# The last two groups of a layer-1 feed-forward issued side by side, the second with its own tiles and PSUM tag

## The chip, the cores and the metric

The kernel runs on one core of one Trainium2 chip. Its engines are TensorE (PE), VectorE (DVE), ScalarE (ACT), GpSimd (POOL) and SyncE (SP)[...]. The metric is the device time of one execution in microseconds, as the median of the runs shown.

## The reference

Two layers, each a graph step and a feed-forward step with a residual, over 32 batches of 512 nodes with 256 features, in float32. The change lies in layer 1's feed-forward and in how it shares time with layer 1's attention. Cut to what matters:

```python
x = x + L0_gnn(layernorm(x), adj)
x = x + L0_ffn(layernorm(x))
x = x + L1_gnn(layernorm(x), adj)      # masked attention, 4 heads of 64, norm per head
x = x + L1_ffn(layernorm(x))

def L1_ffn(x):                          # 8 heads of 64, 64 slices per head
    fx = heads(x @ W_fx.T + b_fx)
    xm = heads(x @ W_x.T + b_x)
    sw = softmax((xm @ W_slice.T + b_slice) / temp)          # nodes x slices
    st = einsum(fx, sw) / (sw.sum(nodes) + 1e-5)             # 64 tokens of 512
    ot = hydra(st)                      # in-projection, convolution, two-way scan,
                                        # gate, RMS norm, out-projection
    out = einsum(ot, sw)                # back to the nodes
    return out @ out_w.T + out_b
```

Every batch is independent of the others; a feed-forward needs the finished attention of its own batch.

## The kernel before

Layer 0 (up to about 2572 us) is untouched. Layer 1 is `layer1_plain`. It has two streams of work, both Python generators whose `yield`s are the points at which the other stream may issue.

**Attention** (`attentions`, L1280): for batch b, `attention(b)` (L1189) is woven with `prepare(b + 1)` (L1121). `prepare` gathers the batch's rows with four indirect DMAs on POOL's queue (L1127), loads and turns the adjacency into a mask (`masks`, L1046), normalizes, transposes (`x3T`), computes the heads (`hp`), adds a bias on POOL (`hv`, L1162) and sends a small row out and back as a broadcast (`own`, L1170 to L1173, SP's queue). `attention` has eight turns; each weighs two heads on DVE (`att`, L1186) and multiplies on PE (`avp`, L1219; `adp`, L1226). Three steps of `norm(b)` (L1254) follow, spread over the next batch's turns; they are DVE work with a power on POOL (L1272).

**Feed-forward** (`mixer(g)`, L1545): a group is two batches, so there are 16 groups, 0 to 15; group 14 is batches 28 and 29, group 15 is batches 30 and 31. For each batch `slices` (L1290) normalizes (`normed`, L1094), transposes (`x4T`), computes logits (`lgp`, L1307), their softmax on ACT and DVE (`sw`, L1308 to L1314), the slice sums (`yTp`, L1319) and the transposed weights (`swp`). Then, for the group, `tokens` (L1330: `uTp`, `rnp`, `uT`) and `scan` (L1355) with its chain `xp`, `bcp`, `dtp`, `zp`, the convolutions and gates, `gp`, `segp`, `mix`, `yp`, `qp`, `y`, `yTp`, `oTp`, `vp`, and for each batch `unslice` (L1534: `outp`, the residual add and the store).

The driver (L1561 to L1569) walks the groups. Each `yield` of a mixer names how many shares of attention work it wants; the shares times `PACE` (1.04 x 2 x 29 / 68 = 0.887) are credited, and for every whole credit one step of attention is issued. The wants of one mixer add up to 68. When attention must wait for a free `x` tile, the credit is cleared. `slices` forces attention on until its own batch is attended. Attention thus runs one or two batches ahead; it ends in group 14, and group 15 has nothing issued beside it.

The order so given is a priority: an instruction whose inputs and tiles are free can be placed in front of one that stands earlier in the program.

All of this uses one SBUF pool, `s1`. Of a mixer's tiles `xn`, `x4T`, `sw`, `uT`, `yT`, `xpad` and `z` have one buffer, `swT` has two, `inner` seven. `v` of a group (L1522) lies in the tag `sw`. In PSUM, pool `p1` has four banks of tag `any`, used by mixers and by `prepare`, and four of tag `pv`, used by `attention`.

Of the kernel before, what the change touches and what calls it, by code (L numbers as in the profile page):

```python
# [8 lines left out]
F32 = mybir.dt.float32  # L9
# [3 lines left out]
AF = mybir.ActivationFunctionType  # L13
# [824 lines left out]
def layer1_plain(tc, ident, eps, x2s, ranks, adj, w, out, over, ps):  # L838
# [35 lines left out]
    with ExitStack() as ctx:  # L874
# [168 lines left out]
        se = ctx.enter_context(tc.tile_pool(name="e1", bufs=2, side="right", reuse_waits="tile"))  # L1043
# [40 lines left out]
        sb = ctx.enter_context(tc.tile_pool(name="s1", bufs=2, reuse_waits="tile"))  # L1084
# [4 lines left out]
        def inner(name):  # L1089
            return sb.tile([P, DI], F32, tag="inner", name=name, bufs=7)  # L1090

        xs, ready, attended, stored = {}, {}, set(), set()

        def normed(xt, xn, name):  # L1094
# [14 lines left out]
        def turned(xn, tag, name, want=None):  # L1109

            xnT = sb.tile([P, DC, N], F32, tag=tag, name=name, bufs=1)
            for c in range(DC):
                pt = psum("any", f"{name}p{c}")
                for t in range(NT):
                    nc.tensor.transpose(pt[:, t * P : (t + 1) * P], xn[:, t, c * P : (c + 1) * P], ident)
                nc.scalar.copy(xnT[:, c, :], pt)
                if c + 1 < DC:
                    yield want
            return xnT

        def prepare(b):  # L1121
# [3 lines left out]
            xt = xs[b] = sb.tile([P, NT, D], F32, tag="x", name=f"x{b}", bufs=AHEAD_X)  # L1125
# [9 lines left out]
            for i, _ in enumerate(edged):  # L1135
                if i < 3 or b not in masked:
                    yield
                if i == 2:
                    normed(xt, xn, f"c{b}")
                    nc.gpsimd.tensor_add(xt, xt, beta.unsqueeze(1).to_broadcast([P, NT, D]))  # L1140
                    yield
            mask = masked.pop(b)
            xnT = yield from turned(xn, "x3T", f"x3T{b}")
# [146 lines left out]
        def slices(b, j, yT, rn):  # L1290


            while b not in attended:
                next(ahead)
            xt = xs[b]
            xn = sb.tile([P, NT, D], F32, tag="xn", name=f"x4{b}", bufs=1)
            normed(xt, xn, f"d{b}")
            yield 5
            xnT = yield from turned(xn, "x4T", f"x4T{b}", 1)
            nc.gpsimd.tensor_add(xt, xt, outb.unsqueeze(1).to_broadcast([P, NT, D]))  # L1300
            sw = sb.tile([P, NT, DI], F32, tag="sw", name=f"sw{b}", bufs=1)
            swT = sb.tile([P, KC, N], F32, tag="swT", name=f"swT{b}")
            yield 2
            for t in range(NT):
                pf = psum("any", f"lgp{b}_{t}")
                for c in range(DC):
                    nc.tensor.matmul(pf, xnT[:, c, t * P : (t + 1) * P], wsl[:, c, :], start=c == 0, stop=c == DC - 1)  # L1307
                nc.scalar.activation(sw[:, t, :], pf, AF.Exp)  # L1308
                nc.vector.tensor_mul(sw[:, t, :], sw[:, t, :], ebsl)  # L1309
                s = sw[:, t, :].rearrange("p (h g) -> p h g", h=H)  # L1310
                st = sb.tile([P, H], F32, tag="sst", name=f"sst{b}_{t}")
                nc.vector.tensor_reduce(st, s, AX.X, ALU.add)  # L1312
                nc.vector.reciprocal(st, st)
                nc.vector.tensor_mul(s, s, st.unsqueeze(2).to_broadcast([P, H, G]))  # L1314
                yield 5 if t + 1 == NT else 1
            for c in range(DC):
                py = psum("any", f"yTp{b}_{c}")
                for t in range(NT):
                    nc.tensor.matmul(py, xn[:, t, c * P : (c + 1) * P], sw[:, t, :], start=t == 0, stop=t == NT - 1)  # L1319
                nc.scalar.copy(yT[:, c, :, j, :], py.rearrange("p (h g) -> p h g", h=H))  # L1320
            for k in range(KC):
                pt = psum("any", f"swp{b}_{k}")
                for t in range(NT):
                    nc.tensor.transpose(pt[:, t * P : (t + 1) * P], sw[:, t, k * P : (k + 1) * P], ident)
                nc.scalar.activation(swT[:, k, :], pt, AF.Identity, accum_out=rn[:, j, k : k + 1])
            nc.vector.tensor_scalar_add(rn[:, j, :], rn[:, j, :], 1e-5)
            nc.vector.reciprocal(rn[:, j, :], rn[:, j, :])
            return swT

        def tokens(g, yT, rn, uT):  # L1330

            pu, pn = psum("any", f"uTp{g}"), psum("any", f"rnp{g}")
            uv, nv = (p.rearrange("p (k j g) -> p k j g", k=KC, j=GB) for p in (pu, pn))
            for k in range(KC):
                for i in range(P // C):
                    half, h = slice(i * C, (i + 1) * C), k * (P // C) + i
                    for c in range(DC):
                        nc.tensor.matmul(uv[half, k], wfxT[:, c, h * C : (h + 1) * C], yT[:, c, h],
                                         start=c == 0, stop=c == DC - 1)
            for k in range(KC):  # L1340
                for i in range(P // C):
                    half = slice(i * C, (i + 1) * C)
                    for j in range(GB):
                        nc.tensor.matmul(nv[half, k, j, :], rn[:, j, k : k + 1].to_broadcast([P, C]), ident[:, half],
                                         start=True, stop=True)
            scale = inner(f"scale{g}")
            nc.scalar.copy(scale, pn)

            for k in range(KC):
                cols = slice(k * GB * G, (k + 1) * GB * G)  # L1350
                nc.vector.scalar_tensor_tensor(uT[:, k, :], pu[:, cols], bfx_eps[:, k : k + 1], scale[:, cols],
                                               ALU.add, ALU.mult)
            nc.vector.tensor_add(uT, uT, bfx.to_broadcast([P, KC, GB * G]))

        def scan(g, uT):  # L1355


            T = GB * G

            def chunks(t):  # L1360
                return t.rearrange("p (k n) -> p k n", k=KC)

            def tok_matmul(p, c0, n):
                for c in range(KC):
                    nc.tensor.matmul(p, uT[:, c, :], inT[:, c, c0 : c0 + n], start=c == 0, stop=c == KC - 1)

            yield 4

            px = psum("any", f"xp{g}")
            for k in range(KC):  # L1370
                for c in range(KC):
                    nc.tensor.matmul(px[:, k * T : (k + 1) * T], inT[:, c, DI + k * P : DI + (k + 1) * P],  # L1372
                                     uT[:, c, :], start=c == 0, stop=c == KC - 1)
            xpad = sb.tile([P, KC, GB, LP], F32, tag="xpad", name=f"xpad{g}", bufs=1)
            nc.gpsimd.memset(xpad[:, :, :, : KW - 1], 0.0)
            nc.scalar.copy(xpad[:, :, :, KW - 1 :], px.rearrange("p (k j l) -> p k j l", k=KC, j=GB))
            pb = psum("any", f"bcp{g}")
            for i in range(2):
                c0 = 2 * DI + i * S
                for c in range(KC):  # L1380
                    nc.tensor.matmul(pb[:S, i * T : (i + 1) * T], inT[:, c, c0 : c0 + S], uT[:, c, :],
                                     start=c == 0, stop=c == KC - 1)
            bpad = sb.tile([S, 2, GB, LP], F32, tag="bpad", name=f"bpad{g}", bufs=1)
            nc.gpsimd.memset(bpad[:, :, :, : KW - 1], 0.0)
            nc.scalar.copy(bpad[:, :, :, KW - 1 :],
                           pb[:S, : 2 * T].rearrange("p (k j l) -> p k j l", k=2, j=GB))

            def conv(src, wts, dst):
                nc.vector.tensor_scalar_mul(dst, src[:, :, 0:G], wts[:, 0:1])
                for q in range(1, KW):  # L1390
                    nc.vector.scalar_tensor_tensor(dst, src[:, :, q : q + G], wts[:, q : q + 1], dst,
                                                   ALU.mult, ALU.add)
# [3 lines left out]
            pd = psum("any", f"dtp{g}")  # L1396
            for j in range(GB):
                for i in range(2):
                    for c in range(KC):
                        nc.tensor.matmul(pd[i * G : (i + 1) * G, j * H : (j + 1) * H],  # L1400
                                         uT[:, c, j * G : (j + 1) * G],
                                         inT[:, c, DT0 + i * H : DT0 + (i + 1) * H],
                                         start=c == 0, stop=c == KC - 1)
# [808 lines left out]
```

## Time and profile before

| | us |
|---|---|
| runs | 4689.87, 4715.24, 4680.16 |
| median | 4689.87 |
| profiled execution | 4695.45 |
| its span, first to last instruction | 4693.7 |
| PE busy in the span | 4097.9 (87%) |
| DVE busy | 3410.9 (73%) |
| ACT busy | 2310.3 (49%) |
| POOL busy | 1747.3 (37%) |

PE is the matmul row; its weight loads are a row of their own and overlap it. A matmul's end is modelled, so a busy PE is not PE at its peak. The granted clock is PE's. "Idle before" in the timeline is the time for which an engine had nothing running ahead of an instruction, with what released it. Three stretches of layer 1's steady part, each about as long as one group takes, look alike:

```profile
4302.00:4435.00 133.00, 123.61 (x729) 73.18 (x728) 94.73 (x200) 63.42 (x162) 38.19 (x28) 0.99 0.18 52
4169.00:4302.00 133.00, 125.69 (x754) 72.90 (x754) 93.49 (x199) 65.78 (x168) 37.66 (x29) 0.99 0.16 50
4036.00:4169.00 133.00, 124.16 (x735) 72.98 (x734) 96.50 (x204) 64.47 (x171) 40.43 (x29) 0.97 0.17 50
```

The columns are the window, its length, the busy time with the number of instructions of PE, weight loads, DVE, ACT and POOL, the granted clock, the DMA engines' mean share and GB/s.

### The profile page before, as it was taken

The numbers are of one execution on the slowest core, as the hardware profiler recorded it, in microseconds if no ns is written. First come the engines' busy times: TensorE is split into PE (matmuls) and PEld (weight loads), VectorE is DVE, ScalarE is ACT, GpSimd is POOL, SyncE is SP. The second block draws the span as 40 slices with busy tenths as digits, with TensorE's granted clock in tenths as the row PEclk, the third lists the DMA queues.
The fourth block names the chain that finished last, engine by engine and source line by source line (L and its number), as shares of the span: only waits on it lengthen the run. The fifth ranks groups of instructions, "written<-read, shape, count | busy, mean of one in ns | idle before, by whom it ended". The sixth has DMA issues, their size and how long they took to land. (4 is left out here: it accounts for less than half of the span.)

```text
span 4693.7 us, 56440 instructions
## 1 busy us (share of the span) xinstructions
PE 4097.9 (87%) x19287; PEld 2514.5 (54%) x19287; DVE 3410.9 (73%) x7232; ACT 2310.3 (49%) x4820; POOL 1747.3 (37%) x2027
## 2 busy tenths in 40 slices
PE   5769887889888899879988899999999999999987
PEld 4545554555555565545554355555555555555555
DVE  6667778777787777867777667777777777777773
ACT  2345555455554555546554444544454554444432
POOL 2363445535456444443443322233333233322220
PEclk8889999999999999989999899999999999999998
DMA  4453445535355343554443211111111111111100
GB/s 123 160 173 104 154 133 165 176 105 163 123 162 173 121 142 107 165 186 143 145 159 113 64 46 45 48 46 52 52 53 55 53 55 55 46 55 55 39 14 15
DMA packets 235101, 474.10 MB, mean 101 GB/s; under 512 B 38299, under 2 KB 114075, under 8 KB 234804
## 3 DMA queue, kind: packets, MB, share of 16 engines
q0 software_dynamic: 80256, 282.38, 19.0%
q1 hardware_dynamic: 154548, 188.02, 12.9%
q8 instruction: 154, 2.52, 0.2%
q14 instruction: 143, 1.17, 0.1%
HBM read 413.16 MB, written 57.16 MB: 100 GB/s over the span
## 5 line engine op out<-in xcount | busy, mean ns | idle before, releaser
L601 PE MATMUL clsp<-xnT,wc 128*128 128x512 f32 x1024 | 530.9, 639 | 92.7 <-ACT cls L603 48.5
L601 PE MATMUL gatep<-xnT,wg 128*128 128x512 f32 x1024 | 505.2, 615 | 32.9 <-ACT gate L603 23.4
L628 PE MATMUL po<-wd,acc 128*128 128x256 f32 x2048 | 456.2, 381 | 20.4 <-DVE xs L630 19.9
L628 PEld LDWEIGHTS po<-wd,acc 128*128 128x128 f32 x2048 | 385.9, 190 | 96.3 <-DVE xs L630 31.8
L1186 DVE SCALAR_TENSOR_TENSOR att<-own,other,mask 128x512 f32<-128x512 f32 x512 | 376.3, 757 | 17.9 <-DMA own<-ownd 16.9
L615 DVE SCALAR_TENSOR_TENSOR acc<-past,fld,acc 128x512 f32<-128x512 f32 x448 | 349.5, 784 | 51.7 <-ACT past L614 38.0
L581 DVE SCALAR_TENSOR_TENSOR best<-rows,xs,best 128x1024 f32<-128x1024 f32 x212 | 276.0, 1304 | 124.5 <-ACT best L575 62.5
L601 PEld LDWEIGHTS gatep<-xnT,wg 128*128 128x128 f32 x1024 | 200.3, 199 | 289.5 <-issue 210.6
L614 ACT ACTIVATE past<-tz,fld 128x512 f32<-128x512 f32 x448 | 293.6, 693 | 97.5 <-DVE acc L615 97.1
L601 PEld LDWEIGHTS clsp<-xnT,wc 128*128 128x128 f32 x1024 | 189.8, 202 | 246.6 <-issue 126.4
L1219 PE MATMUL avp<-att,hv 128*64 128x512 f32 x1024 | 309.8, 628 | 3.3 <-DVE att L1186 3.3
L578 POOL DMA_INDIRECT rows<-table,xs x212 | 253.8, 1197 | 109.4 <-DVE best L581 49.5
L414 PE MATMUL pm<-h,adj 128*128 128x257 f32 x1024 | 268.1, 403 | 28.3 <-DVE u L411 18.5
L1307 PE MATMUL lgp<-wsl,x4T 128*128 128x512 f32 x512 | 253.1, 630 | 33.6 <-DVE mask L1058 26.2
L603 ACT ACTIVATE cls<-clsp,fld 128x512 f32<-128x512 f32 x256 | 176.1, 688 | 215.3 <-PE clsp L601 111.0
L1319 PE MATMUL yTp<-sw,x 128*128 128x512 f32 x512 | 244.1, 617 | 36.8 <-DVE sw L1314 29.6
L1127 POOL DMA_INDIRECT x<-x2s,ranks x128 | 141.3, 1104 | 346.9 <-DVE att L1186 128.5
L617 DVE TENSOR_TENSOR acc<-acc,cls 128x512 f32<-128x512 f32 x256 | 180.6, 707 | 94.3 <-ACT acc L610 88.6
L603 ACT ACTIVATE gate<-gatep,fld 128x512 f32<-128x512 f32 x256 | 175.2, 684 | 149.7 <-PE gatep L601 118.2
L610 ACT ACTIVATE acc<-tz,fld 128x512 f32<-128x512 f32 x256 | 199.0, 779 | 96.4 <-PE tz L608 90.8
L533 POOL DMA_INDIRECT xs<-rows_of,order x128 | 146.5, 1144 | 264.6 <-DVE acc L615 118.3
L414 PEld LDWEIGHTS pm<-h,adj 128*128 128x128 f32 x1024 | 201.1, 202 | 77.8 <-DVE u L411 25.6
(597 smaller groups left out, 8999.1 us busy)
## 6 DMA issues: line engine op xcount, KB each, us to landing
adji<-in_adj SPq DMA_DIRECT2D x128, 256.0 KB, 4.5
ai<-in_adj SPq DMA_DIRECT2D x128, 256.0 KB, 2.7
own<-ownd SPq DMA_DIRECT2D x128, 256.0 KB, 3.7
rows_of<-keep SPq DMA_DIRECT2D x32, 550.0 KB, 6.7
x<-in_x SPq DMA_DIRECT2D x32, 512.0 KB, 7.6
x2s<-xs SPq DMA_DIRECT2D x32, 512.0 KB, 2.9
out<-x SPq DMA_DIRECT2D x32, 512.0 KB, 3.2
rows<-table,xs POOLq DMA_INDIRECT x212, 5.4
```

The costliest lines, as they stand in the source:

```text
L414: nc.tensor.matmul(pm[:, : D + 1], a[:, i, t * P : (t + 1) * P], h[:, i, :], start=i == 0, stop=i == NT - 1)
L578: nc.gpsimd.indirect_dma_start(out=row, out_offset=None, in_=table, in_offset=bass.IndirectOffsetOnAxis(ap=idxs[:, k : k + 1].bitcast(U32) ...
L581: nc.vector.scalar_tensor_tensor(m, row, vals[:, k : k + 1], m, ALU.add, ALU.max)
L601: nc.tensor.matmul(pf, wf[:, c, f * P : (f + 1) * P], xnT[:, c, :], start=c == 0, stop=c == DC - 1)
L603: nc.scalar.activation(o, pf, fn, bias=fld[:, f, bf : bf + 1], scale=1.0 if fn == AF.Gelu else 0.5)
L614: nc.scalar.activation(r, z, AF.Relu, bias=fld[:, f, AT + b : AT + b + 1])
L615: nc.vector.scalar_tensor_tensor(y, r, fld[:, f, CH + b : CH + b + 1], y, ALU.mult, ALU.add)
L628: nc.tensor.matmul(po[:, :D], acc[f][:, t * P : (t + 1) * P], wd[:, f, :], start=f == 0, stop=f == FC - 1)
L1186: nc.vector.scalar_tensor_tensor(e, own[h], other[:, j, h : h + 1], mask[:, j, :], ALU.max, ALU.mult)
L1219: nc.tensor.matmul(pv[q][k * HO : (k + 1) * HO, :], hv[:, j, h, :HO], weighed[b, h, j], start=j == 0, stop=j == NT - 1)
L1307: nc.tensor.matmul(pf, xnT[:, c, t * P : (t + 1) * P], wsl[:, c, :], start=c == 0, stop=c == DC - 1)
L1319: nc.tensor.matmul(py, xn[:, t, c * P : (c + 1) * P], sw[:, t, :], start=t == 0, stop=t == NT - 1)
```

## The change

Four things, all in `layer1_plain`:

1. The pool is split. `s1` (now `sm`) keeps `x` and the mixers' tiles; a new pool `a1` (`sb`) takes attention's. `a1` and the mask pool `e1` are entered on a stack of their own, `early`, which is closed when attention has ended.
2. `slices`, `tokens`, `scan`, `unslice` and `mixer` move into a function `mixers(sb, bank)`, which takes the pool and the PSUM tag; their bodies are the same, with `psum(bank, ...)` for `psum("any", ...)`. `normed` and `turned` get the pool (and the tag) as arguments.
3. In group 14 attention is credited at twice `PACE`. When attention is exhausted, the loop over group 14's steps is left where it stands.
4. Attention's pool is closed, a pool `s2` is opened in its place, and the rest of group 14 is issued step by step in turn with group 15 (`braid`, L90), which uses `s2` and the tag `pv`.

```diff
-        se = ctx.enter_context(tc.tile_pool(name="e1", bufs=2, side="right", reuse_waits="tile"))
+        early = ctx.enter_context(ExitStack())
+        se = early.enter_context(tc.tile_pool(name="e1", bufs=2, side="right", reuse_waits="tile"))
...
-        sb = ctx.enter_context(tc.tile_pool(name="s1", bufs=2, reuse_waits="tile"))
+        sm = ctx.enter_context(tc.tile_pool(name="s1", bufs=2, reuse_waits="tile"))
+        sb = early.enter_context(tc.tile_pool(name="a1", bufs=2, reuse_waits="tile"))
...
-        def slices(b, j, yT, rn):
+        def mixers(sb, bank):
+            def inner(name):
+                return sb.tile([P, DI], F32, tag="inner", name=name, bufs=7)
+            def slices(b, j, yT, rn):
...
-                pf = psum("any", f"lgp{b}_{t}")
+                    pf = psum(bank, f"lgp{b}_{t}")
...
+            return mixer
...
         ahead = attentions()
-        credit = 0.0
-        for g in range(B // GB):
-            for want in mixer(g):
-                credit += want * PACE
-                while credit >= 1.0:
+        credit, over_with = 0.0, object()
+        mixer = mixers(sm, "any")
+        last = B // GB - 1
+        for g in range(last):
+            steps_ = mixer(g)
+            for want in steps_:
+                credit += want * (PACE if g + 1 < last else 2.0 * PACE)
+                state = None
+                while credit >= 1.0 and state is not over_with:
                     credit -= 1.0
-                    if next(ahead, True):
+                    state = next(ahead, over_with)
+                    if state:
                         credit = 0.0
+                if state is over_with:
+                    break
+        for _ in ahead:
+            pass
+        early.close()
+        sm2 = ctx.enter_context(tc.tile_pool(name="s2", bufs=2, reuse_waits="tile"))
+        braid(steps_, mixers(sm2, "pv")(last))
```

`braid` takes one step of each live stream in turn:

```python
def braid(*streams):

    live = [iter(s) for s in streams]
    while live:
        live = [s for s in live if next(s, live) is not live]
```

## The prediction

> **What bounds the kernel now.** I read the windows view first, cut where the trace changes character: start of group 14, last attention transposes, start of group 15's matmuls, its token step, its last matmul. Columns: window, us, then busy us (instructions) of PE, weight loads, DVE, ACT, POOL, then granted clock, DMA share, GB/s.
>
> ```profile
> 4443.00:4536.50 93.50, 87.47 (x491) 43.18 (x489) 73.19 (x163) 39.84 (x91) 23.24 (x18) 1.00 0.07 23
> 4536.50:4580.00 43.50, 31.02 (x185) 27.11 (x186) 21.32 (x37) 8.84 (x19) 8.61 (x5) 0.76 0.04 13
> 4580.00:4616.50 36.50, 33.81 (x95) 15.57 (x94) 17.00 (x35) 12.96 (x27) 2.35 (x1) 0.95 0.04 15
> 4616.50:4679.20 62.70, 50.86 (x373) 42.42 (x371) 17.91 (x54) 21.68 (x41) 0.71 (x1) 0.84 0.03 9
> 4443.00:4679.20 236.20, 203.16 (x1139) 128.28 (x1137) 129.42 (x287) 83.32 (x176) 34.91 (x25) 0.91 0.05 16
> ```
>
> PE is the bound as long as attention runs (87.5 of 93.5 us); after it PE idles 12.5, 2.7 and 11.8 us in the three windows and the clock drops. The timeline of PE shows where:
>
> ```profile
> 4535.26 1.04 PE L1205 MATMUL bp<-ident,avT 128*128 128x128 f32 x8
> 4543.15 3.28 PE L1484 MATMUL yp<-xk,mix 64*64 64x64 f32 x32 [6.85 <-DVE mix L1477]
> ...
> 4553.04 1.08 PE L1499 MATMUL yTp<-ident,y 128*128 128x128 f32 x4 [4.81 <-DVE y L1494]
> 4554.80 6.47 PE L1507 MATMUL oTp<-yT,hoT 128*128 128x128 f32 x32 [0.68 <-ACT yT L1501]
> ...
> 4565.55 14.08 PE L1539 MATMUL outp<-v,swT 128*128 128x256 f32 x64
> ...
> 4580.74 7.13 PE L1307 MATMUL lgp<-wsl,x4T 128*128 128x512 f32 x16 [0.24 <-ACT x4T L1116]
> ...
> 4600.84 8.83 PE L1307 MATMUL lgp<-wsl,x4T 128*128 128x512 f32 x16 [0.57 <-ACT x4T L1116]
> ...
> 4623.82 5.44 PE L1372 MATMUL xp<-uT,inT 128*128 128x128 f32 x32 [2.65 <-DVE uT L1353]
> ```
>
> Two stalls of group 14 (6.85, 4.81) stand bare although group 15's slices were ready: batch 30's statistics ran at 4527. Its logits start only after the last outp: `sw` has one buffer, and `v` of group 14 sits in it until outp has read it. Slow matmuls follow each stall: oTp 6.47 against 3.84 in group 13, xp 5.44 against 3.84 in group 14, the second lgp 8.83 against 7.13. The timeline of DVE shows the other half:
>
> ```profile
> 4477.85 0.26 DVE L1573 TENSOR_TENSOR over<-edges 128x128 f32<-128x128 f32 x1
> ...
> 4538.44 0.68 DVE L1476 TENSOR_TENSOR mix<-mix,back 128x512 f32<-128x512 f32 x1
> 4539.04 1.22 DVE L1262 SCALAR_TENSOR_TENSOR av<-av,ht 128x1024 f32<-128x1024 f32 x1
> 4540.17 2.83 DVE L1477 TENSOR_TENSOR mix<-mix,decay 128x512 f32<-128x512 f32 x1
> ```
>
> L1573 stands last in the program, yet runs at 4478: ready work is pulled into gaps unless tiles hold it back. L1477 takes 2.83 where group 15's takes 0.69; a POOL add (L1300) runs from 4539.03 for 3.42.
>
> **What the Trainium skill says.** "TensorE: Matmul & The Clock Gate", Part 1: an idle window of about 3.4 us halves PE's clock. Agrees: 0.76 in the window with the 6.85 gap. "Perfetto Trace Analysis", Identifying Performance Opportunities: bubbles can mean that the next tile has no buffer. Agrees: `sw`/`v`. The same page, Optimizing Scalar/DVE Operations: GpSimd and DVE share an SBUF read port. Agrees: 2.83 against 0.69. "ScalarE: Activation LUTs", What ACT_TABLE_LOAD costs: 1283 ns plus a drain of about 1380. The trace has 1.28 a load; the next ACTIVATE follows at once, so I price a switch at 1.28.
>
> **The change, part by part.** Loss against warm, gapless PE from 4443 to 4679.2: idle 33.0 (236.2 - 203.2) plus cold excess: oTp 2.6, x4T31 0.9, lgp 1.7, xp 1.6, oTp 2.3, segp and xtp 0.5 = 9.6. So warm PE work is 193.6 and loss 42.6: front 6.0; group 14's tail 12.5 + 2.6 = 15.1; slices 30/31 2.7 + 2.6 = 5.3; group 15's tail 11.8 + 4.4 = 16.2.
>
> *Moved: attention to double pace.* Counting yields, 49 attention steps remain at the start of group 14 in either version. Before, they are spent at `yp y` of group 14; now at its 14th yield, after batch 29's last logits: both slices carry all attention. Rows, 4441 to 4557: att 19.9, av 4.0, three norms 26.5, masks 2.7, statistics 2.4, hv 1.5, small 1.0 = 58.0 DVE; two slices 17.7 + 2.8 = 20.5; batch 27's last adds 1.6, flags 1.4. DVE sum 81.5. PE: avp 18.8, adp 8.5, hp 4.4, transposes 7.0, slices without batch 29's yTp and swp 28: 67; behind the last norm those 9.4 and tokens 3.4 can still go: 80. So **DVE becomes the bound of the front half**. It idled 20.3 of 93.5 before, on batch 31's gather (3.7), the POOL add into `hv` (8.2), POOL powers (4.9), dp (1.8). With more ready work I halve that: 81.5 + 10 = 92, attention over near 4535, front PE idle 12. Ends: 4 (as dense as 4462 to 4478, without a DVE gap) and 22 (all gaps kept, 101.8 - 80). POOL's share (four gathers, two adds of 2.4 to 3.4, pows of 3.3 to 4.4), the mask loads and the `own` write and reads on SP's queue (3.4 + 4.5) crowd into the same stretch: inside those ends.
>
> *Added: second set, `pv` banks, braid.* No instruction is added on PE, DVE or POOL. Group 14's tokens to outp alternate with batch 30's slices and the start of batch 31's. Its 15.1 and the slices' 5.3 should be filled: each gap below 7 us meets a 7 us lgp or yTp of the other stream. I keep 4 (the slices still wait once for their normed x, and norm 31 ends there); ends 1 and 9. ACT switches tables more: up to 8 loads, 10 us, but ACT is busy 9 of 43 us there: nothing on PE; bare, 2.6 us in the 4. The new tiles lie where attention's were and wait for its last readers: norm 31, in front of them in DVE's queue anyway; zero, at most its 2.4 (L1275, L1276). Two out stores of 3.2 us move between the slices on SP; nobody waits for them since no gather is left.
>
> *Kept:* group 15's tail, 16.2; nothing is left to run beside it.
>
> *Elsewhere:* up to group 13 the order is the same by count. The split of one pool in two puts attention's tiles on other addresses, so other tiles of layer 0 hold them back at the border (PE idles 18 us of 2550 to 2600): zero, 5 either way.
>
> Sum: loss after 12 + 4 + 16.2 = 32.2, against 42.6: **10 us less**. The profiled execution was 4695.45 (span 4693.7 and 1.75 around it), 5.6 above the median 4689.87: 4685 there, 4680 as a median.
>
> **Rivals.**
> *Front pays it all*: idle there 18 to 22; gain 0 ± 4: 4690. For: DVE at 81.5 of 92. Against: pulled work as at L1573.
> *Front filled*: idle near 4, the braid pulling a little of group 15's tail forward: gain 16 to 30: about 4667. Against: the gather and `own` chain of batch 31 has fixed latencies.
> *Slower*: DVE's queue stands at batch 31's first att for the `own` reads (3.4 + 4.5 = 7.9), which now follow attention 30 with one mixer step between; batch 28's softmax and norm 30 queue behind it. DVE gaps then are 20.3 + 7.9 = 28.2, attention over at 4553, front idle 30: loss 50, 4697. It decides from an idle front of 22.4 (42.6 - 4 - 16.2), attention ending past 4545. For: DVE waited so at 4434 (3.03, before it 5.77). Against: PE can fill it with group 14's xp to zp, some 12 us.
> *Not doing what it says*: the shared addresses hold group 15 back until attention's last tiles are free and order is then as before: no braid gain, front loss 6: 4696. Against: attention ends before the braid starts.
>
> **How the numbers follow.** About 1% (47 us) is what a measurement here tells from no change; all loss above is 42.6, so faster by 1% would need a gain elsewhere: 0.02. Forecast (gain 4 to 16) 0.47; front filled 0.15; front pays all 0.20; slower or not braided (4694 to 4712) 0.16; outside 0.02. Runs of before lie from 4680 to 4715, which adds some 8 on each side. Likeliest alone: 4672 to 4688. Range 4660 to 4704. Slower by 1% needs twice the bare stalls priced: 0.04; same 0.94.
>
> **What would show it.** PE timeline: batch 30's lgp before group 14's outp; no gap over 3 us between 4540 and group 15's tokens; oTp of group 14 near 3.8. DVE above 85% until the last L1276, that before 4545. Group 15's tail again near 62 us. Wrong if lgp of batch 30 still follows outp, if DVE's front gaps exceed 20, or if the change lies before 4443.

## The result and the profile after

| | before | changed |
|---|---|---|
| median of 12 runs each | 4691.74 | 4695.88 |
| lowest to highest | 4680.16 to 4715.24 | 4682.90 to 4700.55 |
| ratio changed / before | | 1.0001, 95% interval 0.9985 to 1.0016 |
| span of the profiled execution | 4693.7 | 4684.0 |
| layer 0: its last store issued at | 2572.5 | 2566.8 |
| **last stretch**: end of group 13's last outp to end of group 15's | 234.8 | 228.9 |

The ratio's interval is -7.0 to +7.5 us: no measurable change. The profiled spans differ by 9.7 us, but 5.7 of them lie in layer 0, where both kernels issue the same code. Runs of one kernel scatter by 18 to 40 us, so the whole time cannot resolve this edit.

I therefore measure every kernel also by the last stretch, which holds all that the change touches except the new addresses of attention's tiles. One kernel profiled twice (e4 and e7 below) gave 222.1 and 221.8 there while its two whole times were 4678.38 and 4699.34. Seven kernels that issue the same up to the end of attention (the changed one, e2, e4 to e7, e11) took 88.2 to 89.6 us from group 13's end to there, and group 15's tail, the same matmuls in ten kernels without a filler, took 59.4 to 61.8. So I read differences from some 3 us on. The changed kernel is 5.9 us shorter in the stretch. In front of the stretch nothing can be read: from layer 0's last store to the end of group 13 it took 1873.6 us against 1871.7 before, but e4 and e7, one kernel, took 1871.1 and 1881.6.

The windows view of the changed kernel, with the columns that the prediction names. The cuts are the end of group 13, the end of attention's last norm, the token step of group 15, the end of its outp:

```profile
4440.40:4530.00 89.60, 80.07 (x343) 33.26 (x341) 70.78 (x125) 29.16 (x72) 22.34 (x16) 0.94 0.08 24
4530.00:4608.20 78.20, 73.37 (x420) 49.29 (x421) 37.17 (x107) 33.77 (x63) 7.80 (x7) 0.96 0.04 14
4608.20:4669.30 61.10, 49.80 (x373) 40.91 (x371) 17.71 (x53) 21.69 (x41) 0.71 (x1) 0.86 0.03 9
4440.40:4669.30 228.90, 203.24 (x1133) 123.46 (x1131) 125.65 (x283) 84.62 (x176) 30.85 (x24) 0.93 0.05 17
```

PE idles 9.5, 4.8 and 11.3 us, 25.7 in all. The kernel before, with the prediction's cuts (4444.2, 4536.5, 4616.5, 4679.0), idles 6.0, 15.2 and 11.6, which is 32.8. By these cuts the middle won 10.3 us of idle time, the front lost 3.5, and PE's busy time rose by 1.3 (203.2 against 202.0) for the same matmuls. The second cut is not the same point in both: 4536.5 is the end of attention's last transposes, and norm 31 of the kernel before ends only at 4558.2. With both cut at these transposes (4536.3 and 4511.0), PE idles 5.8 and 5.3 us ahead of them, and 15.4 and 9.1 from there to group 15's tokens. The sum holds for any cut, the split does not. The timeline of PE shows the middle and the tail:

```profile
4548.15 2.74 PE L1312 MATMUL lgp<-wsl,x4T 128*128 128x512 f32 x6
4552.51 0.45 PE L1464 MATMUL gp<-cpad,bcT 64*64 64x64 f32 x8 [1.63 <-ACT cpad L1439]
...
4554.40 4.46 PE L1312 MATMUL lgp<-wsl,x4T 128*128 128x512 f32 x10
4558.79 1.90 PE L1489 MATMUL yp<-xk,mix 64*64 64x64 f32 x32
...
4566.65 3.84 PE L1512 MATMUL oTp<-yT,hoT 128*128 128x128 f32 x32 [0.56 <-ACT yT L1506]
...
4579.41 7.07 PE L1544 MATMUL outp<-v,swT 128*128 128x256 f32 x32
...
4615.52 5.44 PE L1377 MATMUL xp<-uT,inT 128*128 128x128 f32 x32 [2.65 <-DVE uT L1358]
4632.92 0.46 PE L1464 MATMUL gp<-cpad,bcT 64*64 64x64 f32 x8 [4.36 <-issue]
...
4642.48 1.09 PE L1504 MATMUL yTp<-ident,y 128*128 128x128 f32 x4 [2.59 <-DVE y L1499]
```

Batch 30's logits (`lgp`) now stand before and after `gp` of group 14, all of them before its `yp`; the stalls of 6.85 and 4.81 are gone, `yp` takes 1.90 instead of 3.28 and `oTp` 3.84 instead of 6.47. Group 15's tail has the same three long waits as before (2.65, 4.36, 2.59). The front shows the price, first on PE:

```profile
4446.82 0.38 PE L1058 MATMUL maskp<-identb,a 128*128 128x128 bf16 x4 [1.87 <-DVE x L1546]
...
4449.55 1.12 PE L1114 MATMUL x4T28p<-ident,x 128*128 128x128 f32 x4 [1.33 <-DVE mask L1059]
...
4453.00 0.47 PE L1114 MATMUL x3T31p<-ident,hv 128*128 128x128 f32 x1 [1.91 <-ACT hv L1105]
4453.40 1.97 PE L1218 MATMUL avp<-att,hv 128*64 128x512 f32 x2
...
4530.57 1.77 PE L1349 MATMUL rnp<-ident,rn 128*64 128x64 f32 x30 [3.00 <-DVE rn L1332]
4534.40 1.68 PE L1114 MATMUL x4T30p<-ident,x 128*128 128x128 f32 x6 [2.06 <-ACT x L1105]
```

and then on DVE, whose queue explains it:

```profile
4446.02 0.43 DVE L1098 BATCH_NORM_STATS2 stc<-x 128x6 f32<-128x256 f32 x1 [2.40 <-DMA x<-x2s,ranks]
4446.36 0.40 DVE L1546 TENSOR_TENSOR x<-x,outp 128x256 f32<-128x256 f32 x1
...
4454.56 3.50 DVE L1185 SCALAR_TENSOR_TENSOR att<-own,other,mask 128x512 f32<-128x512 f32 x2
...
4527.55 1.23 DVE L1274 TENSOR_TENSOR av<-av,mu 128x1024 f32<-128x1024 f32 x1 [3.01 <-POOL mu L1271]
4528.81 1.22 DVE L1275 TENSOR_TENSOR x<-x,av 128x1024 f32<-128x1024 f32 x1
4529.95 0.16 DVE L1331 TENSOR_SCALAR rn<-rn 128x4 f32<-128x4 f32 x1
```

Read it as a queue. At 4446.02 the statistics of batch 31 have waited 2.40 us for the gather; behind them stands group 13's residual add, whose PSUM bank PE needs, and PE waits 1.87. At 4454.56 two attention weights take 3.50 us, where an undisturbed pair takes 1.41, while a POOL add (L1139) runs from 4454.50 for 2.35. The matmuls they feed come one head at a time (x2) at 1.97, where two heads together (x4) take 1.08. Part of that is PE's clock, as the windows view shows:

```profile
4440.40:4448.90 8.50, 5.94 (x40) 2.05 (x38) 4.10 (x11) 2.03 (x5) 2.69 (x3) 1.00 0.37 110
4448.90:4459.20 10.30, 7.75 (x17) 2.45 (x17) 9.52 (x13) 3.49 (x6) 3.59 (x3) 0.50 0.04 13
4459.20:4530.00 70.80, 66.38 (x287) 28.77 (x286) 57.16 (x103) 23.64 (x61) 16.05 (x10) 1.00 0.05 16
```

A head alone at the full clock took 1.07 (at 4492.52); the step from there to 1.97 goes with the granted clock of 0.50. No wait of PE in this front up to 4459 is longer than 1.91, so the idle window of about 3.4 us that the prediction quotes was not needed here. The kernel before has such a slow pair too (3.44 at 4458.22, beside the same POOL add), but batch 28's logits lie around it on PE, and its clock is 1.00 throughout this front.

At 4527.55 DVE has waited 3.01 for the power of norm 31. The input of batch 29's `rn`, which is all that `rnp` needs, was complete at 4527.19, but `rn` stands behind the norm's last two operations of 1.2 us each: PE waits 3.00.

### The profile page after: what moved, and what is told of

It is laid out like the page before. It is cut to its first block, busy times and chain, and to the rows that moved or that the text cites. A ratio compares the mean times of both kernels' runs of the same rounds, so it can differ in the third digit from the quotient of the medians.

```text
span 4684.0 us, 56439 instructions
## 1 busy us (share of the span) xinstructions
PE 4095.1 (87%) x19287; PEld 2510.3 (54%) x19287; DVE 3414.1 (73%) x7232; ACT 2311.3 (49%) x4820; POOL 1741.4 (37%) x2027
## 5 line engine op out<-in xcount | busy, mean ns | idle before, releaser
L628 PE MATMUL po<-wd,acc 128*128 128x256 f32 x2048 | 456.2, 381 | 14.5 <-DVE xs L630 13.8
L414 PE MATMUL pm<-h,adj 128*128 128x257 f32 x1024 | 266.8, 402 | 28.4 <-DVE u L411 18.8
L1324 PE MATMUL yTp<-sw,x 128*128 128x512 f32 x512 | 249.9, 629 | 39.3 <-DVE sw L1319 32.2
```

What stands on the lines that cost most here:

```text
L414: nc.tensor.matmul(pm[:, : D + 1], a[:, i, t * P : (t + 1) * P], h[:, i, :], start=i == 0, stop=i == NT - 1)
L628: nc.tensor.matmul(po[:, :D], acc[f][:, t * P : (t + 1) * P], wd[:, f, :], start=f == 0, stop=f == FC - 1)
```

## The experiments

All diffs are against the changed kernel unless said otherwise. "Stretch" is the last stretch of one profiled execution. Where no ratio is given, the kernel was run once and only the stretch is read.

### The parts of the change one by one

**e1, old pace.** Braid, second set and `pv` stay.

```diff
-                credit += want * (PACE if g + 1 < last else 2.0 * PACE)
+                credit += want * PACE
```

> Group 14 credits attention at the old pace; the braid with its second set of tiles stays. Measured on the last stretch, from the end of group 13's last outp matmul to the end of group 15's: 234.8 us before, 228.9 changed. Theory 1 (the braid earns some 15 us and the doubled pace gives back some 9): PE's front up to attention's end is as good as before (about 6 us lost), but the two stalls of group 14 in front of yp and yTp (6.85 and 4.81) stay, since they lie beside attention's last norm; only oTp to outp meet batch 30's slices. Stretch 225 to 230. Theory 2 (the doubled pace costs nothing, the braid earns only about 6 in all): less is left to braid, stretch 231 to 234.

Stretch 232.3, in the second range, only 2.5 below before, which is too little to read. The stalls of 4.71 and 4.81 stay bare, as the first expectation had it, although a second set and its banks are there. The DVE timeline of this kernel says why:

```profile
4555.90 1.23 DVE L1275 TENSOR_TENSOR x<-x,av 128x1024 f32<-128x1024 f32 x1
4557.04 0.75 DVE L1098 BATCH_NORM_STATS2 std<-x 128x6 f32<-128x256 f32 x2
```

Batch 30's statistics start when norm 31's last add ends. With the mixer tiles left in the old set (e10 below) they start at 4525.53, 28.5 us before that kernel's norm 31 ends. The set `s2` lies where attention's tiles lay, so group 15 cannot begin before the last of them is free. That the tile addresses are what holds it is inferred from this pair. The doubled pace is thus what makes the place free in time: this way of finding room needs it.

**e2, double pace, no second set, no braid:** group 15 after group 14, on the old tiles and banks.

```diff
-        braid(steps_, mixers(sm2, "pv")(last))
+        for stream in (steps_, mixer(last)):
+            for _ in stream:
+                pass
```

> Doubled pace in group 14, but then group 14 to its end and group 15 after it, both in the one set of tiles and the any banks: no braid, no second set. Theory 1: the doubled pace leaves group 14's chain as bare as group 15's (16 us lost), lgp of batch 30 waits for outp again: stretch 241 to 247, slower than before by 6 to 12. Theory 2: stretch 233 to 237.

**e11, double pace and second set, no braid.**

```diff
-        braid(steps_, mixers(sm2, "pv")(last))
+        for stream in (steps_, mixers(sm2, "pv")(last)):
+            for _ in stream:
+                pass
```

> As changed (doubled pace, second set, pv banks), but group 15 is issued after group 14 and not in turn with it. Theory A: tiles and banks are what counts, ready work is drawn forward into group 14's gaps by itself, group 14's outp comes later only if it ranks lower, so stretch 226 to 232, near the changed kernel's 228.9. Theory B: near dense without braid, 244 to 252.

Stretches 252.1 and 239.6; the first was expected at 241 to 247, the second fell between its two ranges. The ladder reads: before 234.8, doubled pace alone +17.3, own tiles and banks -12.5, step-by-step issue -10.7, together 228.9. Each step rests on one execution. Of the pace's 17.3, 6.1 are idle time and 11.2 slower matmuls (PE busy 213.2 against 202.0 for the same 1131 records): the clock is granted at half for 61 us of e2's stretch and for 44 of before's. The pace costs far more than the front's idle time, because attention was also the cover of group 14's own chain. With attention gone the chain is bare, in the PE timeline of e2:

```profile
4531.73 6.27 PE L1377 MATMUL xp<-uT,inT 128*128 128x128 f32 x32 [6.14 <-DVE uT L1358]
...
4549.93 0.46 PE L1464 MATMUL gp<-cpad,bcT 64*64 64x64 f32 x8 [4.32 <-ACT cpad L1439]
```

In the kernel before, `xp` and `gp` of group 14 had attention matmuls beside them and waited for nothing. So 17 of the 23 us that tiles, banks and braid earn only pay back what the pace took.

### What held batch 30 back: the tile or the bank

The prediction's reading was that batch 30's logits wait because `v` sits in `sw`'s one buffer. These kernels use the old pace and issue group 15 after group 14, as the kernel before does. First `v` alone gets a tile of its own (e8); then `pv` alone (e9); then both (e10).

```diff
+        apart = []
...
-                v = sb.tile([P, NT, DI], F32, tag="sw", name=f"v{g}", bufs=1)
+                v = (apart or [sb])[0].tile([P, NT, DI], F32, tag="sw", name=f"v{g}", bufs=1)
...
-                credit += want * (PACE if g + 1 < last else 2.0 * PACE)
+                credit += want * PACE
...
-        sm2 = ctx.enter_context(tc.tile_pool(name="s2", bufs=2, reuse_waits="tile"))
-        braid(steps_, mixers(sm2, "pv")(last))
+        apart.append(ctx.enter_context(tc.tile_pool(name="s2", bufs=1, reuse_waits="tile")))
+        for stream in (steps_, mixer(last)):
+            for _ in stream:
+                pass
```

> Old pace in group 14 and no braid, groups one after the other in one set of tiles, but v gets a tile of its own in attention's place, so that it no longer sits in sw. Tests the prediction's reading that batch 30's logits wait for outp because of the one sw buffer. If sw was what held them, ready work is drawn forward by itself: lgp of batch 30 starts before group 14's outp, stretch 228 to 232 against 234.8 before and 232.3 with single pace and braid. If the order of issue is what counts: lgp of batch 30 still after outp, 234 to 236.

Stretch 234.8, to the tenth that of the kernel before, as the second expectation had it. Its PE timeline has the old order:

```profile
4565.11 14.08 PE L1546 MATMUL outp<-v,swT 128*128 128x256 f32 x64
4579.02 1.04 PE L1114 MATMUL x4T30p<-ident,x 128*128 128x128 f32 x8
4580.30 7.13 PE L1314 MATMUL lgp<-wsl,x4T 128*128 128x512 f32 x16 [0.24 <-ACT x4T L1115]
```

Even the transposes `x4T30p`, which touch no `sw`, start when outp ends, although their input was ready 40 us earlier: ACT's four normalizing operations ended at 4538.6. What they do need is a PSUM bank. The next kernel leaves `v` in `sw` (the lines with `apart` undone) and gives group 15 the other tag (diff against e8):

```diff
-        for stream in (steps_, mixer(last)):
+        for stream in (steps_, mixers(sm, "pv")(last)):
```

> Old pace, groups one after the other, one set of SBUF tiles, v in sw as before; only group 15's PSUM tiles come from the pv banks. With v apart and the any banks, batch 30's transposes (x4T, which need no sw) still stood behind group 14's outp. Theory A (the any banks are handed out in order of issue, so batch 30's first bank is one that group 14's outp must leave first): x4T of batch 30 now starts before outp; its logits still wait for sw, so the stretch gains little: 231 to 235, against 234.8. Theory B (the order of issue alone holds them): x4T still after outp, 234 to 236.

Stretch 230.4, lower than 231 to 235. The PE timeline:

```profile
4536.20 1.91 PE L1114 MATMUL x4T30p<-ident,x 128*128 128x128 f32 x8 [1.24 <-ACT x L1105]
4538.67 1.98 PE L1312 MATMUL lgp<-wsl,x4T 128*128 128x512 f32 x4 [0.56 <-ACT x4T L1115]
...
4562.46 14.08 PE L1544 MATMUL outp<-v,swT 128*128 128x256 f32 x64
4580.73 2.94 PE L1324 MATMUL yTp<-sw,x 128*128 128x512 f32 x4 [4.19 <-DVE sw L1319]
```

The transposes moved from 4579 to 4536 and the logits stand before outp. Only now does `sw` show: the logits lie finished in four `pv` banks until `v` is read, and `yTp` waits 4.19 for the softmax behind outp.

> As e9_pv_only, and v in a tile of its own. Theory A (bank first, then sw): lgp of batch 30 starts before outp of group 14, in the gaps before yTp and after it, without any braid: stretch 226 to 231. Theory B (order of issue): 234 to 236, lgp after outp.

Both together (e8 with that line): stretch 224.7, below the 226 to 231 expected. The `yTp` wait is gone:

```profile
4544.19 8.20 PE L1314 MATMUL lgp<-wsl,x4T 128*128 128x512 f32 x12
...
4563.07 14.08 PE L1546 MATMUL outp<-v,swT 128*128 128x256 f32 x64
4576.99 6.17 PE L1326 MATMUL yTp<-sw,x 128*128 128x512 f32 x14
```

So one tag and one tile, without the doubled pace, a second mixer set or a braid, give 10.1 us where the whole change gives 5.9, each in one execution. The bank is the first holder (-4.4 alone, 0 for the tile alone), the tile the second (-5.7 once the bank is free). That `any` hands its four banks out in program order, so that batch 30's first bank is one which group 14's last uses must leave, is inferred from these runs and not seen directly. The other tag also brings four more banks; whether more banks of tag `any` would have done the same was not tried.

**e5, the change with one tag for both streams:**

```diff
-        braid(steps_, mixers(sm2, "pv")(last))
+        braid(steps_, mixers(sm2, "any")(last))
```

> As changed, but group 15 too takes its PSUM tiles from the four any banks; the pv banks stay idle after attention. Changed kernel's last stretch 228.9 us, with 5.9 us more PE loss between 4530 and 4594 than a gapless PE. If the second set of SBUF tiles is what makes the braid and banks are no limit: 228 to 231. If four banks for two streams are too few (each bank waits for its copy by ACT or DVE before PE can take it again): PE gaps released by ACT copies appear beside the braid, 233 to 240.

Stretch 238.1, in the second range, 9.2 worse than the change and 3.3 worse than before. `gp` waits 3.88 instead of 1.63 and `yp` 2.11 instead of nothing. Those waits are named after the chain's own operations; what is missing beside them are batch 30's logits, which now come one bank's worth (x4) at a time, at 4541.95, 4549.09, 4552.23 and 4557.94, the last behind `oTp`. That the two streams wait for each other's banks is inferred: the tag is all that was changed. The separate tag carries more than the whole net gain.

### When attention ends

**e3, doubled pace only from the fifth yield of group 14**, to spare the front:

```diff
-            for want in steps_:
+            for n, want in enumerate(steps_):
...
-                credit += want * (PACE if g + 1 < last else 2.0 * PACE)
+                credit += want * (PACE if g + 1 < last or n < 4 else 2.0 * PACE)
```

> As changed, but the doubled pace begins only at group 14's fifth yield, after its first logits. Tests whether the loss in the front half is the gather of batch 31: in the changed kernel PE idles 1.87, 1.33 and 1.91 us between 4446 and 4453 with masks and batch 28's transposes behind a DVE queue that waits for that gather, and then runs avp and adp at half clock. Theory 1a (gather at the start): those gaps go and the stretch falls by 4 to 8, to 221 to 225. Theory 1b (DVE is simply full and the loss moves): stretch 227 to 231.

Both expectations missed: 238.5. The three waits at the start of the front give way to one of 3.42 for a mask (4455.38) and one of 1.55 (4465.50): up to attention's last transposes PE idles 6.1 us against 5.3. A long one is new. From the PE and the DVE timeline:

```profile
4538.60 5.55 PE L1377 MATMUL xp<-uT,inT 128*128 128x128 f32 x32 [9.01 <-DVE uT L1358]
```

```profile
4534.39 1.23 DVE L1274 TENSOR_TENSOR av<-av,mu 128x1024 f32<-128x1024 f32 x1 [2.75 <-POOL mu L1271]
```

Norm 31 now ends just where group 14's tokens begin, 94.9 us after group 13's end instead of 89.6, and the `uT` operations stand behind it in DVE's queue, at a place where PE has nothing else. The inputs of all four were complete at 4530.2; the first ran at 4531.29, the second only behind the norm at 4535.53, although DVE idled 2.75 us between them. Where the attention stream ends decides which short operation is caught behind its last norm.

### Work that nobody waits for, as filler

Group 15's tail idles 11.3 us with nothing beside it. Group 14's outp feeds only its own add and store. **e4 and e7, group 14's outp issued after group 15's `yp` step:**

```diff
-        braid(steps_, mixers(sm2, "pv")(last))
+        behind = mixers(sm2, "pv")(last)
+        for _ in range(8):
+            next(steps_)
+            next(behind)
+        for _ in range(11):
+            next(behind)
+        braid(steps_)
+        braid(behind)
```

> As changed, but group 14's two outp blocks (64 matmuls, 14.1 us of PE, nobody waits for them) are issued after group 15's yp step in place of beside batch 31's transposes. Tests whether group 15's tail, 61 us in both kernels with some 11 idle and 5 of half clock, is bound by its chain only for want of ready PE work. If so: outp falls into the gaps after uT, zp and y, the tail's gaps go, stretch 214 to 222. If ready work is drawn into the first gap it finds: outp runs before the tail as now, stretch 227 to 231.

> e4_late_outp once more, timed in rounds, to see how well the stretch repeats (222.1 us then) and whether its gain of 12.7 us over before shows in the whole time. If it does: stretch 221 to 223, ratio 0.997 to 0.998 with 1 wholly outside or at the edge of the interval. If the rest of the kernel's variation hides it: interval holds 1.

The stretch is 222.1 and 221.8, at the upper edge of what was expected first; in 22 runs of e7 the ratio to before is 0.9974 (0.9962 to 0.9986), median 4684.08. Of outp's 64 matmuls 18 are pulled forward at once, 14 go in at 4601, ahead of `xp`, and 32 between 4616 and 4625, around `gp` and `segp`.

**e6, also `vp` of group 14 behind group 15's token step:**

```diff
-        braid(steps_, mixers(sm2, "pv")(last))
+        behind = mixers(sm2, "pv")(last)
+        for _ in range(7):
+            next(steps_)
+            next(behind)
+        for _ in range(9):
+            next(behind)
+        next(steps_)
+        for _ in range(3):
+            next(behind)
+        braid(steps_)
+        braid(behind)
```

> As e4_late_outp, but group 14's vp step as well is issued only after group 15's token step, so that outp can't be drawn forward into batch 31's transposes (18 of its 64 matmuls were, at 4578). If the tail is only short of ready PE work, some 4 us more of it lie in the tail's gaps and the waits before yp (3.33) and yTp (2.59) shrink: stretch 217 to 221 against 222.1. If those waits come after every filler is used up whatever its order, or batch 31's transposes then stand bare: 222 to 226. Whole time against before: ratio 0.996 to 0.998.

Stretch 215.5, better than the 217 to 221 expected; ratio to before 0.9968 (0.9958 to 0.9979), median 4678.19 of 21 runs against 4691.92. That is some 0.3% below before. Against the changed kernel the comparison is indirect: the interval of its own ratio to before (0.9985 to 1.0016) lies wholly above this one. The idle time of group 15's tail falls from 11.3 us to 6.9 in e7 and 2.4 here. The tail in its PE timeline:

```profile
4611.55 1.99 PE L1544 MATMUL outp<-v,swT 128*128 128x256 f32 x8
4613.38 3.73 PE L1377 MATMUL xp<-uT,inT 128*128 128x128 f32 x32
...
4632.59 4.91 PE L1544 MATMUL outp<-v,swT 128*128 128x256 f32 x22
4637.43 1.90 PE L1489 MATMUL yp<-xk,mix 64*64 64x64 f32 x32
```

The wait for `uT` (2.65) is covered by the last of `vp` and by outp, the wait before `gp` (4.36) by outp, and `xp` runs at 3.73 instead of 5.44. The granted clock over `xp` is 1.00 here and 0.69 in the changed kernel: this filler pays twice, for the gap and for the clock behind it.

**e12, the same with the triple pace** (diff against e6):

```diff
-                credit += want * (PACE if g + 1 < last else 2.0 * PACE)
+                credit += want * (PACE if g + 1 < last else 3.0 * PACE)
```

with the braid's turns counted so that attention's earlier end in the order of issue leaves them in the same place.

> As e6_late_vp_outp (stretch 215.5), with three times the pace in group 14, so that attention ends at group 14's eighth yield and batch 29's slices are left for the braid. In e3_late_ramp a later attention cost 9.6 us, since group 14's token step stood behind the last norm on DVE. If an earlier one gains by the same token (the last norm beside slices instead of the token step): stretch 208 to 214. If PE starves in the first half, DVE alone being fed: 218 to 226.

Stretch 222.8, 7.2 worse; ratio to before 0.9981 (0.9971 to 0.9991), as the second expectation had it. `yTp` of a slice waits 6.09 for the softmax in DVE's queue. Attention ends earlier only in the order of issue: in time norm 31 ends 93.6 us after group 13's end, against 88.2 in e6, and PE idles 13.8 us up to there against 8.8. So this run does not test an earlier end; it shows that a higher pace did not bring one.

The three timed kernels also test the stretch as a measure. Their stretches are some 19.3, 13.0 and 12.0 us below before's; 4691 times one minus the ratio gives 15.0, 12.2 and 8.9, and each stretch, as a ratio (0.9959, 0.9972, 0.9974), lies within its interval. The change's 5.9 would be a ratio of 0.9987, which its interval holds. But in all four the whole time gained less than the stretch, by 1 to 6 us. Whether the split pool costs something in front of the stretch (the prediction's "zero, 5 either way") stays open: 13 executions with it took 1862 to 1882 us from layer 0's last store to group 13's end, 1871.1 in the mean, and the one without it 1871.7.

## Why the prediction came out as it did

The loss against warm PE (without gaps, at a granted clock of 1), in the prediction's terms and over the stretch (warm work 202.0 - 9.6 = 192.4): before 42.4, forecast 32.2, measured 228.9 - 192.4 = 36.5. The gain was 5.9 in the stretch where 10 was forecast. In the whole time the interval allows a gain of 7.0 at most: it holds 0 and 5.9, and not the 10. The median of 4695.88 lies within the range given and above its likeliest part, 4672 to 4688. That the profiled execution came at 4685.80, where 4685 was forecast, is luck, since 5.7 of its 9.7 us come from layer 0.

- **The front's end: right, by two errors that cancel.** Attention was to end near 4535; it ended at 4530.03, which is 4533.8 when group 13's end is laid on that of before. But DVE's idle time was not halved: it was 18.8 us, not 10, after 20.3 before. And DVE was busy 70.8 us, not 81.5: the prediction added up durations, and records that follow each other overlap. Added up in the same way, this front's operations give 79.5. DVE was at 79% and not above 85%. Of its idle time 10.0 us were waits for POOL, 4.8 for the gather and the `own` reads and 3.7 for ACT: such waits set the pace of this front, and "DVE becomes the bound" did not come true.
- **The front's price: too low.** "Front PE idle 12" was priced as idle time alone. Idle was 9.5, below that, but matmuls also stretched: two single heads of `avp` took 1.97 each and one of `adp` 1.70. At the normal 1.08 for two heads and 1.06 for four they would take 0.54, 0.54 and 0.27. That is 4.3 more, so at least 13.8. By a head's time alone at full clock (1.07, and 1.04 for `adp`), some 1.8 of the 4.3 come from heads that came singly and 2.5 from the clock.
- **The middle: right in kind, too low in size.** 4 was kept, 4.8 was idle; no gap over 3 us was left after 4540, and `oTp` ran at 3.84. Seven of `x4T30p` at 2.1, where all eight took 1.0, and `rnp` 0.6 slower came on top, small slow groups after the two waits around 4530. Front and middle together lost some 21.5 (36.5 less the tail's 15) where 16 was forecast; what the front does not account for, up to 7.7, is the middle's.
- **The tail: kept, as forecast.** From `uTp` on it took 59.4 against 60.7. The 1.3 came from a warm `yp` and `qp` (2.2 less), partly lost in a slower `segp` and `oTp` (1.97 and 6.73 against 1.37 and 6.16). So its loss was about 16.2 - 1.3, near 15. The forecast's warm sum had taken `yp` at 3.28 for its normal speed, so the same 2.2 in group 14 was not on its list of gains either.
- **"`sw` has one buffer, and `v` of group 14 sits in it": fell as the first cause.** A tile of its own changes nothing (e8); the PSUM tag was in front of it, and `sw` comes only second (e9, e10). So "Agrees: `sw`/`v`" did not hold as it was read: the buffer that was lacking first was a PSUM bank. The prediction had seen that batch 30's statistics ran at 4527 and that ready work is pulled forward, but did not ask why `x4T30p`, which needs no `sw`, also waited for outp. The forecast survived because the change moves both.
- **The rivals.** The slower one needed DVE to stand at batch 31's `own` reads: DVE waited 0.5 us for them (4485.19), and attention ended well before 4553. "Shared addresses hold group 15 back" was right as a mechanism, as far as e1 and e10 let it be inferred, but with doubled pace attention is over when group 15 starts, as the prediction's counter-argument said. "Front pays it all" put the gain at 0 ± 4 and the forecast at 4 to 16: the stretch's 5.9 lies in the lower part of the forecast, and the front idle of 9.5 is not that rival's 18 to 22. The whole time alone could not tell the two apart.

Left open: the arrangement of e10 with group 14's outp kept as a filler for group 15's tail. The two gains lie in different parts of the stretch, but their sum was not tried. No run took the POOL add away from the slow pair of attention weights either.

The tail's longest wait, 4.36 us before `gp`, has a cause that no run touched. The profile puts it down to "issue", but `gp` starts 0.09 us after ACT has finished `cpad`, which it reads. ACT's timeline of the changed kernel, its first and last lines:

```profile
4623.26 1.28 ACT L1432 ACT_TABLE_LOAD   x1
...
4629.77 1.28 ACT L1427 ACT_TABLE_LOAD   x1
...
4632.44 0.39 ACT L1439 ACTIVATE cpad<-bcT,bc_b 64x128 f32<-64x128 f32 x1
```

ACT works through this chain almost without a gap and loads tables five times in it, as Silu, Exp, Silu, Ln and Silu follow each other: 6.4 us in all. Another order of these functions, with fewer loads, was not tried.

## What to carry to other kernels

When ready work is not drawn into a gap, find the first operation of it that waits, and ask for each thing this operation takes, the PSUM bank of its tag included; a free tile behind a held bank shows nothing. Hurrying one stream to make room for another also removes it as cover: price the chain it used to cover, not only the stretch into which it is pressed. Work whose result nobody waits for can fill a last latency chain (here the stretch fell from 228.9 to 215.5). An edit worth a tenth of a per cent is judged on the stretch that it touches, once it is known how well that stretch repeats. And durations of one engine's records are not simply added up: here 79.5 us of them were 70.8 us of busy time.

## What the runs showed of the hardware

Two DVE operations over 128x512 took 3.50 and 3.44 us where a POOL add over 128x1024 ran beside them, and 1.41 otherwise; "Perfetto Trace Analysis", Optimizing Scalar/DVE Operations, in the Trainium skill names the port that the two engines share. These numbers fit it; no run took the POOL add away. PE's granted clock was 0.50 from 4448.9 to 4459.2 in the changed kernel, in a front whose longest wait up to there is 1.91 us. A POOL power over 128x16 took 2.9 to 5.3 us. The same program took 4678.38 and 4699.34 us in two executions whose last stretches agree to 0.3 us: of the 21 us between them, 10.7 arise in layer 0 and 10.5 from its last store to the end of group 13.
